# A graph attention layer with a mixture of experts: the general attention as a second pass behind the experts, and a new opening

## The chip, the cores and the metric

The kernel runs on one core of a Trainium2 chip. The metric is the device time of one execution in microseconds. The engines named below are TensorE (PE), VectorE (DVE), ScalarE (ACT), GpSimd (POOL) and SyncE (SP); each works through its own instructions in order, and SP, ACT and POOL also issue DMA transfers.

## What is computed

`x` has 4096 rows of 256 numbers, `adj` is a 4096 x 4096 matrix of 0 and 1, which the kernel gets transposed. A graph attention layer with four heads of 64 is followed by a layer of eight experts, of which each row uses its best two.

```python
# attention on n = layernorm(x); h, s_col, s_row come from n
h = jnp.einsum('nd,hdk->hnk', x, W)
s_col = jnp.einsum('hnk,hk->hn', h, a1)
s_row = jnp.einsum('hnk,hk->hn', h, a2)
e = jax.nn.leaky_relu(s_row[:, :, None] + s_col[:, None, :], negative_slope=0.2)
e = jnp.where(adj[None, :, :] > 0, e, NEG_INF)
att = jax.nn.softmax(e, axis=-1)
h_prime = jnp.einsum('hij,hjk->hik', att, h)
y = jax.nn.elu(out) + x @ Wr + br           # out: h_prime, heads side by side
x = x0 + layernorm(y) * gamma + beta        # x0: the layer's input
# experts on n = layernorm(x)
top_w, top_i = jax.lax.top_k(n @ Wg + bg, 2)     # softmax over the two
for e in range(8):
    hid = jax.nn.gelu(n @ W1[e] + b1[e], approximate=False)
    out = out + w_dense[:, e:e + 1] * (hid @ W2[e] + b2[e])
```

## The kernel before

**Stages.** An opening, the attention, the experts. The rows are cut into eight blocks of 512 (`b`, each of four tiles of 128). The attention goes over four groups of 1024 target rows (`a`), each of two halves of one block, and in each over 32 tiles of 128 source rows (`j`). For each `j` and head VectorE makes a weight tile `w` of 128 x 1024 (`weigh`, L1353), and TensorE multiplies it into the sums `acc` (L835) and the denominators `den` (L844): 24 products a step, 12 where only one half is done. Ten `w` buffers lie between the two engines.

**Separable and general form.** Where the scores stay within a limit, exp(leaky_relu(r + c)) is the larger of two products of a row factor and a column factor, so `w` is one instruction: maximum of the row factor `er` and the column factor `eb`, then minimum with the mask. Where they do not, a general form is used (maxima over the neighbours first, then the weights). Which of the two it is depends on a limit found from the weights (`scores_weights`, L551 to L557, ends in `flag`). The flag is read by every engine (L1270) and `tc.If(general > 0)` (L1275) stands in front of both forms. With these inputs the general form is never taken.

**Opening.** `norm_block(0)`: statistics, three root steps, normalised rows (L623), transposes (L630), copies that also sum the columns (L643). `scores_weights` makes the score columns of the weights by a product and a reduction on VectorE. `project_first` multiplies block 0 (L747), `store_parts` and `load_rows` (L793, L800) send its row factors through memory so that each partition gets all of them (`er`). `residual_first` (L778) computes the residual of block 0. Block 1 is normalised ahead of the branch.

**Behind the branch.** For the first four `j` the halves are done one by one, half 0 and then half 1, because block 1 has to be projected first (L695, L702) and its row factors go through memory too; `prepare_at` gives out this work. Block 2 is normalised and projected during the half-1 steps (its first piece is at step 4), blocks 3 to 7 at steps 4b to 4b+3. From `j = 4` on both halves are done. Between the steps the results of the group before are finished (`pending`). In the last group the list of the first expert tiles is made (`plan_early`, `first_tile`).

**Experts.** For each tile of an expert `fetch`, `turn`, `up` (L1519) and `down` (L1550); the sum `o` (L1561) is added into the output by an indirect DMA on POOL (L1572). Each add waits for the add before it. The last tile's two adds (`o_last0`, `o_last1`) are held back: the first (L1556) goes out when its own sum is ready, the second (L1572) behind it. A count of tiles that did not fit the plan is read, and `tc.If(further > 0)` (L1645) guards tiles beyond the fixed number; it is not taken either. The generator `giving` of the last tile is finished behind that branch: the second half's sum and add.

Of the kernel before, what the change touches and what calls it, by code (L numbers as in the profile page):

```python
# [32 lines left out]
WARM = 37  # L33
# [10 lines left out]
def gat_then_moe(  # L44
# [92 lines left out]

    def rows_of(mat, b):
        return mat[ts(b, B), :].rearrange("(t p) d -> p t d", p=P)
# [15 lines left out]
    def root_of(var, n, part=1.0, steps=3):  # L155


        v = small.tile([P, n], F32, tag="v", name="v")
        nc.vector.tensor_scalar(v, var, part, EPS, op0=OP.mult, op1=OP.add)
        r = small.tile([P, n], F32, tag="r", name="r")  # L160
        nc.vector.tensor_scalar(
            r.bitcast(I32), v.bitcast(I32), -0.5, 1597463007.0, op0=OP.mult, op1=OP.add
        )
        q = small.tile([P, n], F32, tag="q", name="q")
        for _ in range(steps):
            nc.vector.tensor_tensor(q, r, r, OP.mult)
            nc.vector.scalar_tensor_tensor(q, q, -0.5, v, op0=OP.mult, op1=OP.mult)
            nc.vector.scalar_tensor_tensor(r, q, 1.5, r, op0=OP.add, op1=OP.mult)
        return r, v
# [27 lines left out]
    moe = ctx.enter_context(tc.tile_pool(name="moe", bufs=1))  # L197
    fin = ctx.enter_context(tc.tile_pool(name="fin", bufs=1))
    ps = ctx.enter_context(tc.tile_pool(name="ps", bufs=1, space=PSUM))
    gam = fin.tile([P, D], F32)  # L200
    bet = fin.tile([P, D], F32)

    hbar = fin.tile([P, H // 2], F32)


    home = [fin]

    def large(name):
        return home[0].tile([P, TB, D], F32, tag="large", name=name, bufs=3)

    def first_large(name):
        return fin.tile([P, TB, D], F32, tag="first", name=name, bufs=2)

    def loaded(name):
        return fin.tile([P, TB, D], F32, tag="loaded", name=name, bufs=2)

    def residuals(name):
        return fin.tile([P, TB, D], F32, tag="residual", name=name, bufs=1)

    def bank(shape, name):  # L220
        return ps.tile(shape, F32, tag="bank", name=name, bufs=3)

    tiny = fin.tile([P, 1], F32)
    nc.vector.memset(tiny, TINY)

    xr0 = moe.tile([CH, 2, RW], F32)
    xT0 = moe.tile([P, DC, TT], F32)
    w10 = moe.tile([P, DC, F], F32)


    b1r = moe.tile([E * FC, P], F32)
    bT = moe.tile([P, FC, E], F32)

    def turn_biases():
        pb = bank([P, E * FC], "pb")
        order_of(nc.tensor.transpose(pb, b1r, ident[: E * FC, : E * FC]))
        nc.vector.tensor_copy(bT, pb.rearrange("p (e f) -> p f e", e=E))

    plans = [moe]

    def moe_tile(name, shape, dtype=F32):
        return plans[0].tile(shape, dtype, name=name, bufs=1)

    def tables(tag, width):

        return {
            "expert": moe_tile(f"expert{tag}", [P, width]),
            "mark": moe_tile(f"mark{tag}", [P, width]),
            "own": moe_tile(f"own{tag}", [P, width, E]),
            "place": moe_tile(f"place{tag}", [P, width]),  # L250
            "rows": moe_tile(f"rows{tag}", [P, width]),
            "float": moe_tile(f"float{tag}", [P, 2, width]),
            "int": moe_tile(f"int{tag}", [P, 2, width], I32),
            "past": moe_tile(f"past{tag}", [P, width, E]),
            "parts": 3 if tag == "w" else 2,
            "upto": moe_tile(f"upto{tag}", [P, E]),
        }

    def whole(name, n, least):

        more = moe_tile(f"more{name}", [P, E, KT])
        less = moe_tile(f"less{name}", [P, E])
        nc.vector.tensor_scalar(less, n, least, None, op0=OP.subtract)
        nc.vector.tensor_tensor(
            more, less.unsqueeze(2).to_broadcast([P, E, KT]),
            steps.unsqueeze(1).to_broadcast([P, E, KT]), OP.is_gt,
        )
        tiles = moe_tile(f"tiles{name}", [P, E])
        nc.vector.tensor_reduce(tiles, more, AX.X, OP.add)
        return tiles  # L270

    def plan(t, width, n, tiles, used):

        wide = [P, width, E]
        upto, past, own, place = t["upto"], t["past"], t["own"], t["place"]
        nc.vector.tensor_copy(upto, tiles)
        for e in range(1, E):
            nc.vector.tensor_tensor(
                upto[:, e : e + 1], upto[:, e : e + 1], upto[:, e - 1 : e], OP.add
            )  # L280
        nc.vector.tensor_tensor(
            past, upto.unsqueeze(1).to_broadcast(wide),
            num[:, :width].unsqueeze(2).to_broadcast(wide), OP.is_le,
        )
        nc.vector.tensor_reduce(t["expert"], past, AX.X, OP.add)
        nc.vector.tensor_tensor(past, past, tiles.unsqueeze(1).to_broadcast(wide), OP.mult)
        nc.vector.tensor_reduce(place, past, AX.X, OP.add)
        nc.vector.tensor_tensor(place, num[:, :width], place, OP.subtract)

        nc.vector.tensor_scalar(  # L290
            t["mark"], t["expert"], -1.0, float(E), op0=OP.mult, op1=OP.add
        )
        nc.vector.tensor_tensor(
            own, t["mark"].unsqueeze(2).to_broadcast(wide),
            order.unsqueeze(1).to_broadcast(wide), OP.is_equal,
        )
        if used is not None:
            nc.vector.tensor_tensor(
                past, own, used.unsqueeze(1).to_broadcast(wide), OP.mult
            )  # L300
            nc.vector.tensor_reduce(t["rows"], past, AX.X, OP.add)
            nc.vector.tensor_tensor(place, place, t["rows"], OP.add)
        nc.vector.tensor_scalar(place, place, float(TT), None, op0=OP.mult)
        nc.vector.tensor_tensor(past, own, n.unsqueeze(1).to_broadcast(wide), OP.mult)
        nc.vector.tensor_reduce(t["rows"], past, AX.X, OP.add)
        nc.vector.tensor_tensor(t["rows"], t["rows"], place, OP.subtract)
        table = t["float"]
        nc.vector.tensor_scalar(table[:, 0], t["expert"], float(E - 1), None, op0=OP.min)
        nc.vector.scalar_tensor_tensor(
            table[:, 1], t["expert"], float(LIST), place, op0=OP.mult, op1=OP.add  # L310
        )

        nc.vector.tensor_scalar(
            table[:, 1], table[:, 1], filled[:, E - 1 :], None, op0=OP.min
        )
        nc.vector.tensor_copy(t["int"], table)
        return t
# [104 lines left out]
    def after(ins, other, reason):  # L422
# [3 lines left out]
            reason=reason,  # L426
        )

    last = [None]

    def queue(ins):

# [1252 lines left out]
```

## Time and profile before

| | us |
|---|---|
| median of 3 runs (lowest, highest) | 1284.34 (1283.99, 1289.04) |
| the profiled execution's time | 1287.53 |
| its span in the profile | 1285.8 |
| its mean granted TensorE clock | 0.996 |
| TensorE busy | 1255.5 |
| VectorE busy | 847.7 |
| ScalarE busy | 463.3 |
| POOL busy | 239.2 |

In the profile an instruction group is given as line, engine, operation, tiles out<-in and shape, then the number of instructions. `DVEq`, `POOLq` and so on are what an engine's sequencer does itself: reads of a register, branches, events. In square brackets stands the idle time in front of an instruction and what ended it. A window's row gives the busy time of each engine in that stretch, the granted clock and the share of the DMA engines.

### The profile page before, as it was taken

What the parts mean: (1) busy time and instruction counts of PE and PEld (TensorE: products, weight loads), DVE (VectorE), ACT (ScalarE), POOL (GpSimd) and SP (SyncE); (2) the same over time, 40 slices, a digit from 0 to 9 for tenths busy, and PEclk for the clock granted to TensorE, in tenths of its full rate; (3) what the DMA queues carried; (4) which work ended last, traced back from release to release, by engine and by line L of the source; (5) the groups of instructions that cost most, each with busy time, mean ns of one, the idle gap of its engine ahead of it and who ended that gap; (6) DMA issues with size and microseconds to landing.
All of it is one profiled execution on the core that took longest, in us unless ns stands there. A gap on an engine that the chain in (4) does not pass through costs nothing.

```text
span 1285.8 us, 23209 instructions
## 1 busy us (share of the span) xinstructions
PE 1255.5 (98%) x9073; PEld 685.4 (53%) x9073; DVE 847.7 (66%) x1623; ACT 463.3 (36%) x974; POOL 239.2 (19%) x196
## 2 busy tenths in 40 slices
PE   6999999999999999999999999998999999999997
PEld 4434444332232332332322325887888877888886
DVE  5799887879999999999999994934111121111110
ACT  4313222155522365421654313532333333233232
POOL 1000000001002701007010042245222212221212
PEclk9999999999999999999999999999999999999999
DMA  6523533336533746335463325978776776787782
GB/s 204 182 84 115 190 107 115 106 134 134 187 110 105 230 112 201 101 99 164 140 176 118 101 71 196 331 200 251 218 189 162 197 183 143 199 209 194 192 210 42
DMA packets 145010, 205.84 MB, mean 160 GB/s; under 512 B 49808, under 2 KB 113952, under 8 KB 144240
## 3 DMA queue, kind: packets, MB, share of 16 engines
q1 hardware_dynamic: 122432, 161.26, 40.8%
q0 software_dynamic: 20224, 35.68, 12.4%
q10 hardware_dynamic: 2224, 7.22, 1.6%
q8 instruction: 76, 1.25, 0.4%
q14 instruction: 54, 0.44, 0.1%
HBM read 171.89 MB, written 29.08 MB: 156 GB/s over the span
## 4 chain that ended last, share of the span: by engine, by line
PE 70%; DVE 6%; DMA 1%; issue 1%; SPq 1%; ACT 0%; POOLq 0%; DVEq 0%; ACTq 0%
PE acc L835 23%; PE po L1550 17%; PE ph L1519 17%; PE den L844 11%; DVE w L1353 4%; DMA early<-lists 1%; PE ptx L890 1%; PE pt L494 1%; PE ptr L1122 0%; PE pl L901 0%; DMA out<-o_last,ids 0%; SPq L1135 0%; SPq L1136 0%; POOLq L1681 0%; PE pd L1038 0%
## 5 line engine op out<-in xcount | busy, mean ns | idle before, releaser
L835 PE MATMUL acc<-w,ha 128*32 128x512 f32 x4096 | 670.4, 594 | 0.9 <-ACT u L1032 0.9
L1353 DVE SCALAR_TENSOR_TENSOR w<-er,eb,am 128x1024 f32<-128x1024 f32 x496 | 604.5, 1276 | 29.4 <-PE den L844 21.9
L844 PE MATMUL den<-w,unit 128*2 128x512 f32 x2048 | 465.5, 594 | 10.7 <-DVE w L1353 9.1
L835 PEld LDWEIGHTS acc<-w,ha 128*32 128x32 f32 x4096 | 182.2, 110 | 297.9 <-issue 265.2
L1236 ACT ACTIVATE am<-adj 128x1024 bf16<-128x1024 int32 x124 | 130.8, 1055 | 362.1 <-DVE w L1353 218.9
L1519 PE MATMUL ph<-xT,w 128*128 128x256 f32 (+1 forms) x1056 | 241.3, 386 | 4.3 <-DVE xT L498 3.1
L1550 PE MATMUL po<-w,hT 128*128 128x256 f32 x1088 | 240.2, 379 | 0.0
L1523 ACT ACTIVATE hT<-ph,bias 128x256 f32<-128x256 f32 (+1 forms) x264 | 126.2, 480 | 294.5 <-PE ph L1519 207.1
L1519 PEld LDWEIGHTS ph<-xT,w 128*128 128x128 f32 x1056 | 200.0, 190 | 40.2 <-DVE xT L498 3.5
L1550 PEld LDWEIGHTS po<-w,hT 128*128 128x128 f32 x1088 | 205.5, 190 | 27.7
L1561 DVE SCALAR_TENSOR_TENSOR o<-po,share,b2s 128x256 f32<-128x256 f32 x66 | 31.8, 482 | 261.0 <-PE po L1550 242.8
L844 PEld LDWEIGHTS den<-w,unit 128*2 128x2 f32 x2048 | 93.5, 85 | 163.0 <-issue 157.2
L1572 POOL DMA_INDIRECT out<-o,ids x66 | 103.0, 1561 | 334.1 <-DVE o L1561 157.3
L1016 POOL DMA_INDIRECT lists<-xe,at x64 | 93.6, 1463 | 267.0 <-issue 182.3
L498 DVE COPY xT<-pt 128x256 f32<-128x256 f32 x12 | 5.1, 424 | 61.3 <-PE pt L494 61.3
L725 POOL DMA_DIRECT2D residual<-rb x7 | 5.5, 779 | 159.2 <-DVE rb L720 136.6
L1542 ACT ACTIVATE b2s<-b2b,share 128x256 f32<-128x256 f32 x68 | 30.8, 503 | 0.0
L695 PE MATMUL ph<-wall,xT 128*128 128x264 f32 x112 | 28.8, 400 | 0.7 <-ACT xT L643 0.7
L695 PEld LDWEIGHTS ph<-wall,xT 128*128 128x128 f32 x112 | 20.0, 189 | 15.1 <-issue 8.7
L1072 POOL DMA_DIRECT2D xf<-in_x x6 | 8.1, 1345 | 100.3 <-ACT xf L1071 54.8
L702 PE MATMUL pr<-wr,xT 128*128 128x256 f32 x112 | 26.5, 379 | 0.0
L1353 DVE SCALAR_TENSOR_TENSOR w<-er,eb,er 128x512 f32<-128x512 f32 x32 | 22.3, 744 | 5.6 <-issue 5.6
(348 smaller groups left out, 632.7 us busy)
## 6 DMA issues: line engine op xcount, KB each, us to landing
w<-in_L_ffn_W SPq DMA_DIRECT2D x66, 1024.0 KB
adj<-in_adj SPq DMA_DIRECT2D x126, 512.0 KB
er<-parts ACTq DMA_DIRECT2D x3, 2048.0 KB
b2b<-in_L_ffn_b SPq DMA_DIRECT2D x33, 128.0 KB
early<-lists SPq DMA_DIRECT2D x16, 260.0 KB
residual<-rb POOLq DMA_DIRECT2D x8, 512.0 KB
rb<-residual SPq DMA_DIRECT2D x8, 512.0 KB
out<-y POOLq DMA_DIRECT2D x8, 512.0 KB
```

The source lines that it names most:

```text
L695: order_of(nc.tensor.matmul(phs[t - t0], xT[:, c, ts(t, P)], wall[:, c, :], start=(c == 0), stop=(c == DC - 1),))
L835: queue(nc.tensor.matmul(acc[half][h // 2][here : here + Q, :], ha[:, j, h * K + g * Q : h * K + (g + 1) * Q], w[half][h], start=(j == 0), ...
L844: queue(nc.tensor.matmul(den[here : here + HB, :], unit[:, j, h, 1 - half : 1 - half + HB], w[half][h], start=(j == 0 and half == 0), stop ...
L1016: ins = nc.gpsimd.indirect_dma_start(lists, bass.IndirectOffsetOnAxis(ap=at[:, k, t : t + 1], axis=0), xe[:, t, :], None,).ins
L1236: nc.scalar.activation(am, at, AF.Relu, scale=2.0)
L1353: nc.vector.scalar_tensor_tensor(wh[:, these], er[:, these, h], eb[:, j, h : h + 1], mask[:, these], op0=OP.max, op1=OP.min,)
L1519: order_of(nc.tensor.matmul(ph, job["w1"][:, c, ts(f, P)], xT[:, c, :], start=(c == 0), stop=(c == DC - 1),))
L1523: job["gelu"] = nc.scalar.activation(hT[:, f, :], ph, AF.Gelu, bias=job["bias"][:, f : f + 1]).ins
L1542: nc.scalar.activation(b2s[k], b2b, AF.Identity, scale=share[:, k : k + 1])
L1550: order_of(nc.tensor.matmul(po, hT[:, f, ts(k, CH)], w2[:, f, :], start=(f == 0), stop=(f == FC - 1)))
L1561: given_out.append(nc.vector.scalar_tensor_tensor(o, po, share[:, k : k + 1], b2s[k], op0=OP.mult, op1=OP.add).ins)
L1572: add()
```

## The change

The attention and the experts move into one function `forward(apart, stack)`. The program calls `forward(True, ctx)`, the separable form, with no branch in front of it. The old flag becomes `strayed`; it is carried into the table of counts, and its maximum with the other two conditions is what the branch at the end reads. In that branch stand the further tiles, and, under a second condition, `forward(False, again)`, the whole general pass, after which the two last sums are set to zero. The two last adds stand behind the branch.

```diff
+    held, further, held_back, last_sums = forward(True, ctx)
+    with tc.If(held(2, 1) > 0):
+        further()
+        with tc.If(held(3, 1) > 0):
+            with ExitStack() as again:
+                held, further, rest_of_sums, _ = forward(False, again)
+                with tc.If(held(2, 1) > 0):
+                    further()
+                for add in rest_of_sums:
+                    add()
+            for o in last_sums:
+                nc.vector.memset(o, 0.0)
+    for add in held_back:
+        add()
...
-    with tc.If(further > 0):
...
-    next(giving, None)
...
             if k + 1 == nch:
                 yield
-                while job["last"] and held_back:
-                    held_back.pop(0)()
             if job["last"]:
-                o = work.tile([CH, D], F32, name=f"o_last{k}", bufs=1)
+                o = kept.tile([CH, D], F32, name=f"o_last{k}")
+                last_sums.append(o)
...
-            if job["last"] and k + 1 < nch:
+            if job["last"]:
                 held_back.append(add)
```

The opening is new. `first_phase(weigh)` writes its instructions in an order by hand, and `in_trace_order` ties each engine to that order. The score weights come from TensorE (`heads_made`, `weights_turned`, `scores_weights`). The rows are only centred before they are transposed, and their factor `r` is applied behind the products (`of_tile`, `scaled`, `residual_kept`). The limits use no root step and a factor of 1.09 in place of one step and 1.01. The row factors of blocks 0 and 1 are spread over the partitions by 16 transposes each and four copies (`spread_parts`), not through memory; blocks 2 to 7 go through memory as before. The column sums of blocks 0 and 1 are 16 products with one moving column (`sums_of_centred`). Block 1's root steps run on POOL. The warm-up products go from 37 to 9 and 3.

```diff
-        warm_up(WARM)
...
-        norm_block(0)
-        second = rows_loaded(1)
-        with tc.issue_after(marks["off"]):
-            scores_weights()
-        project_first()
...
-        with tc.If(general > 0) as chosen:
...
+            def sums_of_centred(xb, r):
+
+                po = bank([P, DC], "po")
+                for c in range(DC):
+                    for t in range(TB):
+                        order_of(nc.tensor.matmul(
+                            po[:, c : c + 1], xb[:, t, ts(c, P)], r[:, t : t + 1],
+                            start=(t == 0), stop=(t == TB - 1),
+                        ))
+                return po
...
+            def spread_parts(part, er):
 
+                for h in range(H):
+                    pe = bank([P, B], "pe")
+                    for t in range(TB):
+                        order_of(nc.tensor.transpose(
+                            pe[:, ts(t, P)], part[:, h, t : t + 1].to_broadcast([P, P]), ident
+                        ))
+                    ins = nc.scalar.copy(er[:, h], pe).ins
+                return ins
...
+            def first_phase(weigh):
...
+                warm_up(9)
+                heads_made()
+                warm_up(3)
...
+                spread_parts(part, er0[:, 0])
+                factors(0, slice(2, TB), scs[0])
...
+                heads_added(0)
+                rb = residuals("rb")
+                sums_first = [residual_products(0, t0) for t0 in (0, 2)]
...
+                for t in range(TB):
+                    centred(second, mvs[1], t)
...
+                roots_of_pool(vs[1], rs[1])
...
+                heads_added(1)
...
+                heads_added(2)
...
+                heads_added(3)
...
+                residual_pair(1, rb, 0)
+                marks["eb"] = spread_parts(part, er0[:, 1])
+                residual_pair(1, rb, 2)
+                nc.gpsimd.dma_start(rows_of(residual, 1), rb)
+                pos = [sums_of_centred(xb, r) for xb, r in ((first, rs[0]), (second, rs[1]))]
+                for b in range(HB):
+                    nc.vector.tensor_copy(sums[:, :, b], pos[b])
+
+            def roots_of_pool(v, r):
+
+                q = small.tile([P, TB], F32, tag="qp", name="qp")
+                for sign in (1, 1, -1):
+                    nc.gpsimd.tensor_tensor(q, r, r, OP.mult)
+                    nc.gpsimd.tensor_tensor(q, q, v, OP.mult)
+                    nc.gpsimd.tensor_scalar(q, q, -0.5 * sign, 1.5 * sign, op0=OP.mult, op1=OP.add)
+                    nc.gpsimd.tensor_tensor(r, r, q, OP.mult)
```

Block 2 is projected during steps 4 to 7 with both halves; so far it was during the half-1 steps. Three groups of VectorE and ScalarE work get a mark behind which they are placed.

```diff
-                    for b in range(1, NB):
-                        first = {1: 0, 2: TB}.get(b, TB * b)
-                        if b > 1 and first - 3 <= s < first:
+                        for b in range(2, NB):
+                            first = TB * b
+                            if first - 3 <= s < first:
...
-                        if first <= s < first + (3 if b == 1 else 4):
+                            if first <= s < first + 4:
...
+                with tc.issue_after(marks["top"]):
+                    found = measured(b, fetched.pop(b))
...
+                with tc.issue_after(marks["eb"]):
                 mask_of(at[:, 0], am)
...
                 for j in range(TB):
-                    am = first_masks[:, j]
-                    if j > 1:
-                        mask_of(first_adj[:, j - 2], am)
-                    attend(weigh(er, am, j, [0]), j, [0])
-                    prepare_at(j)
-                    if j == 2:
-                        load_rows(er[:, 1:], 1, 1, nc.sync)
-                for j in range(TB):
                     prepare_at(TB + j)
                     attend(weigh(er, first_masks[:, j], j, [1]), j, [1])
```

In the built program's order VectorE has, behind its copy of the column sums, the rest of the half-1 `w`, the statistics of block 2 and six `w` of the steps 4 and 5 ahead of block 2's row offset (`off`). TensorE has block 2's transposes ahead of the last half-1 step. On SP the loads of the last blocks' residuals and rows, which stood behind the end of the branch's region, stand among the adjacency loads. The first of the last two adds waits for VectorE's event behind the jump over the branch, because the block that is jumped over writes the sums too.

## The prediction

> **What bounds the kernel now.** I read the busy shares first, then the windows of the opening and of the join between attention and experts, then two timelines of the opening, and last the chain and the branch at the very end.
>
> ```profile
> PE 1255.5 (98%) x9073; PEld 685.4 (53%) x9073; DVE 847.7 (66%) x1623; ACT 463.3 (36%) x974; POOL 239.2 (19%) x196
> ...
> L1353 DVE SCALAR_TENSOR_TENSOR w<-er,eb,am 128x1024 f32<-128x1024 f32 x496 | 604.5, 1276 | 29.4 <-PE den L844 21.9
> ```
>
> TensorE sets the time over almost the whole span. A shift of its stream early on is carried to the end, because a full attention step costs TensorE 24 instructions of 0.2146 us, 5.15 us, against four w on VectorE at a pitch of 1.2 us, 4.8 us. So only the places where TensorE is idle can give time: the opening, the join and the end.
>
> ```profile
> 10.00:20.00 10.00, 8.51 (x45) 5.95 (x43) 8.28 (x44) 6.13 (x14) 0.00 (x0) 1.00 0.68 260
> 20.00:30.00 10.00, 3.83 (x22) 3.21 (x20) 3.76 (x11) 4.32 (x10) 0.79 (x1) 0.92 0.50 167
> 30.00:40.00 10.00, 9.16 (x44) 4.75 (x48) 9.29 (x25) 3.33 (x6) 0.00 (x0) 0.74 0.82 275
> ...
> 50.00:60.00 10.00, 7.23 (x48) 4.13 (x40) 3.92 (x10) 3.76 (x10) 0.00 (x0) 1.00 0.49 164
> ...
> 29.28 3.40 DVE L1353 SCALAR_TENSOR_TENSOR w<-er,eb,er 128x512 f32<-128x512 f32 x5 [5.59 <-issue]
> ...
> 30.84 1.02 PE L844 MATMUL den<-w,unit 128*2 128x512 f32 x2 [7.00 <-DVE w L1353]
> ...
> 54.86 0.17 DVE L711 TENSOR_TENSOR sc<-ph,limits 128x8 f32<-128x8 f32 x1 [4.61 <-PE ph L695]
> ```
>
> In a window row the columns are PE, PEld, DVE, ACT and POOL busy, clock, DMA share, GB/s. The first gap is the branch: the row factors' load leaves at 22.42, all engines resume at 29.0 to 29.3, and TensorE starts attention at 30.84 after 7.0 us. The clock is then low: 0.50 in 30 to 34, 0.68 in 34 to 36. The second gap, 51.2 to 59.5 with a block's projection in it, is block 1's factors going through memory. From 72.1 (first step with both halves) TensorE is full, and block 2 has been projected by then.
>
> ```profile
> 790.00:800.00 10.00, 8.68 (x48) 7.40 (x47) 5.00 (x32) 3.10 (x8) 0.00 (x0) 1.00 1.01 351
> ...
> 810.00:820.00 10.00, 8.73 (x47) 7.59 (x46) 9.72 (x36) 5.53 (x8) 1.22 (x2) 1.00 1.06 339
> ...
> L1645 DVEq EVENT_SEMAPHORE  x2: 21/21/21, 1277.7 to 1277.8; - x2
> ...
> L1645 POOLq COMPARE_BRANCH  x1: 53/53/53, 1266.1 to 1266.1; - x1
> ...
> L1645 DVEq COMPARE_BRANCH  x1: 72/72/72, 1274.8 to 1274.8; - x1
> ...
> 1274.39 0.49 DVE o_last L1561
> 1274.88 0.27 issue
> 1275.15 3.72 DMA out<-o_last,ids
> ...
> 1277.95 0.48 DVE L1561 SCALAR_TENSOR_TENSOR o_last<-po,share,b2s 128x256 f32<-128x256 f32 x1 [3.08 <-DVEq L1645]
> ```
>
> At the join TensorE loses 1.32 and 1.27 us while the DMA share is above 1. At the end the first held-back add leaves at 1275.15, as soon as its own sum is there. VectorE's jump, compare at 1274.8 and its next event at 1277.7, lies under TensorE's last product, which ends at 1277.73.
>
> **The opening, part by part.** Removed: the flag's read and branch, seven idle us; two products and two reductions of 0.69 and 0.68 on VectorE; block 0's and block 1's trips through memory (a 1 MB load each). Added on TensorE: score weights (a few transposes of 0.13 us), 32 transposes that spread the row factors, and 16 products with one moving column (column sums, so far an accumulating output of ScalarE's copies).
>
> First attention product. Rows arrive at 5.4 as now (5.47). Four statistics pairs (0.43 and 0.18), weights copied by ScalarE (0.60), centred rows (0.59 each) and their transposes bring the first projection to 10.9, the limits' chain to 13.7 (dependent small operations every 0.20), scores and factors to 16.05, spread transposes and four copies of 0.60 to 17.4 to 19.05, first w at 17.45: TensorE at about 18.9 instead of 30.84.
>
> TensorE's work from there to the end of the new opening, in its built order: four half steps of 2.58 (10.3); residual products of two blocks, 2 x 3.64 (half a projected pair with its residual takes 1.82: 64.79 to 66.61); eight transposes 1.05; block 1's products 3.76 (two pairs of 1.88); 16 spread transposes 2.1; 16 column products. The trace has no row of this last kind; the nearest is the limits' product, also 128x128 weights and a few columns, 0.31 us an instruction. From below a transpose bounds it (0.13), from above two weight loads of 0.19. I take 0.31: 5.0 us (2.1 to 6.1). Sum 29.5: the opening's last product ends at 48.4, and VectorE's copy of the sums, which waits for it, at 48.8.
>
> What is late next. VectorE is in order, and behind that copy it has, before it makes block 2's row offsets: 11 half w (0.665 each, 7.3), block 2's statistics (2.3), 11 small root operations (1.9), then six full w of the steps j=4 and j=5 (7.2), a statistic of block 3 and the offset itself (0.6). That is 19.3 us, so 68.1. TensorE's order puts block 2's transposes in front of the last half-1 step. It has only three half steps and runs dry near 56 to 58. ScalarE normalises four rows by 70.2, the last transposes take 0.25, the half step 2.58: the first full step can start at 73.0, against 72.1. The idle ten us are longer than the 7.0 that were followed by half clock for about 4 us; the first 1.5 us of that are transposes paced by ScalarE, and the rest costs 1.35. So 74.4. And block 2, now projected in j=4 to 7, still owes two pairs of 3.70 (62.91 to 66.61): 7.4. The opening costs 74.4 + 7.4 - 72.1 = **+9.7 us**.
>
> Bounds: if VectorE never waited, its work from 17.45 to the offset (32 half w 21.3, six full 7.2, statistics 5.1, small ones 4.6, 14 operations of 0.42 for ha and residuals 5.9) is 44 us, offset at 61.5, first full step at 66.4 warm: +1.7. From above: the 12 root operations now on POOL have no row there beside a DMA issue and its memsets; at 0.13 to 0.67 each (an iota, and an estimate five times that) they add 0 to 2: +11.7.
>
> The clock in the new opening is a cost of its own. The 37 warm-up products become 12, and before, the product pitch falls from 0.43 to 0.21 only at 4.6. A page speaks against the cut: the Trainium skill, "TensorE: Matmul & The Clock Gate", Part 1, has the clock fall to half after one idle window of about 3.4 us and rise only after about 3.4 us of sustained work, and the sparse products of 6 to 19 us might not be that. By the rule the opening could be half-clocked there; by the trace's row for the first 30 us (0.92 to 1.00) it is not.
>
> **The join.** No branch region ends there, so the loads of the last blocks' residuals and rows (2 MB) go earlier, between adjacency loads on SP; each is behind a store that ended several steps before, and an adjacency tile has about 15 us of slack (three mask buffers of 5.15), which hides it. TensorE loses about 3 us around 790 to 820 now. Bounds -3 to +1 (a copy and one more wait on VectorE); I take **-1**, since the weights' own loads still fill the DMA.
>
> **The end.** Both last sums now come ahead of the branch, and both adds behind it. The block that is jumped over writes those sums too, so the built add waits for VectorE's event behind the jump. POOL is queued behind that wait with both adds. VectorE's last sum runs 1277.95 to 1278.43; its read of the count takes 0.4 beside it (1274.4 to 1274.8 now), compare to event 2.9, POOL's issue 0.2: the first add leaves at 1281.4 instead of 1275.15, and the second and the span's end follow it: **+6.2 us**. From below POOL's own jump took 0.4 us (its next event is at 1266.5; +3.7), from above TensorE's 3.9 (+7.2). A page would price it otherwise: the Trainium skill, "Advanced Engine Details and Errata", Control Flow Timing, gives a compare-and-branch about 108 ns, which would make the end +3.5 and the total about 1296.5. VectorE's own 2.9 us decides.
>
> Sum: 9.7 - 1.0 + 6.2 = +14.9. Against the profiled execution (1287.53, span 1285.8, 1.7 around it) that is 1302.4. That execution lies 3.2 above the median of the runs shown, 1284.34, so against the median it is 1299.2.
>
> **Rivals.** A: VectorE sets the new opening without waiting, as at the lower bound. For it: VectorE is 80% busy in the first 100 us, and its w may run ahead of TensorE. Against: its sums copy sits behind TensorE's last opening product. 1284.3 + 1.7 - 1 + 6.2 = 1291.2.
>
> B, the other side: TensorE never runs dry in the opening. This needs block 2's offset before about 56. Then 48.4 + four half steps 10.3 + transposes 1.05 + owed 7.4 = 67.2, which is -4.9; with join and end as above 1284.6, and 1280 if both are at their lower bounds. For it: the branch's seven us are really gone. Against: 11 half and six full w stand ahead of the offset.
>
> C: half clock between 6 and 19. Some 7 us of TensorE work lie there on the chain; at 0.5 they cost 3.5 to 7: 1303 to 1306.
>
> D: the jump is short, as POOL's: 2.5 less, 1296.7, inside the forecast.
>
> **How the numbers follow.** The forecast with D, 1293 to 1303, has 0.52; A 0.22; B 0.14; C 0.12. The time is the forecast's, 1299. The range 1287 to 1305 takes in A, most of C and leaves out most of B and a rest. About 0.5%, 6.4 us, is what a measurement can tell: same is 1277.9 to 1290.8. Faster: the low end of B with the first add released earlier than I read it, 0.04, and 0.01 for the rest. Same: what is left of B (0.10), half of A (0.11) and 0.02 of the forecast, 0.23. Slower: 0.72.
>
> **What would show it.** Opening: first attention product near 19; a wait of block 2's transposes on ScalarE of some 10 us before 70; the first full step near 74 with block 2's projection behind it; a low clock around 70. End: the first add some 3 us behind the last sum, released by VectorE's queue. The forecast is wrong if that gap is under 3 us, if TensorE's first full step comes before 67, or if the idle time at the join grows.

## The result and the profile after

| | before | after | difference |
|---|---|---|---|
| median of 4 runs each (lowest, highest), us | 1285.63 (1283.99, 1289.04) | 1302.64 (1302.38, 1303.19) | ratio 1.0129, 95% interval 1.0106 to 1.0152 |
| profiled execution: time, span | 1287.53, 1285.8 | 1302.63, 1301.0 | +15.2 in the span |
| first attention product begins | 30.84 | 19.21 | -11.6 |
| end of the first attention group | 266.75 | 274.06 | +7.3 |
| TensorE's last product ends | 1277.73 | 1286.26 | +8.5 |
| span ends | 1285.8 | 1301.0 | +15.2 |

The new kernel is slower. Read downwards, the last column tells where: attention begins 11.6 us earlier, by the end of the first group the kernel is 7.3 us behind, between there and the last product 1.2 us are added, and 6.7 more behind it. The end of the first group is read from one product that has the same idle time in front of it in both kernels. Here are its lines, from TensorE's timelines of the kernel before and, in the second fence, of the kernel after (start, duration, engine, line; the idle time and its releaser in brackets):

```profile
266.75 0.62 PE L835 MATMUL acc<-w,ha 128*32 128x512 f32 x2 [0.93 <-ACT u L1032]
```

```profile
274.06 0.62 PE L1090 MATMUL acc<-w,ha 128*32 128x512 f32 x2 [0.92 <-ACT u L1287]
```

I call the time from the first attention product to this one the first group. It was 235.91 us and is now 254.85: 18.9 us more, of which 11.6 had been won ahead of it. It holds more work than before (projections and residuals that used to lie ahead of the first product), but the windows of the kernel after show that work is only part of it:

```profile
40.00:50.00 10.00, 9.90 (x78) 8.19 (x80) 6.76 (x14) 4.99 (x7) 0.78 (x1) 1.00 0.30 87
50.00:60.00 10.00, 7.00 (x60) 1.90 (x52) 9.16 (x25) 0.00 (x0) 0.00 (x0) 1.00 0.63 229
60.00:70.00 10.00, 2.47 (x12) 1.36 (x16) 9.65 (x30) 3.61 (x6) 0.00 (x0) 0.51 0.16 52
70.00:80.00 10.00, 10.00 (x74) 2.58 (x67) 7.15 (x9) 3.79 (x9) 0.00 (x0) 0.81 0.32 100
```

TensorE (first column after the width) is full until 57, busy for 2.47 us of the ten from 60 to 70, and then runs at a granted clock of 0.81 on average. VectorE (third) is full in just that stretch. The timeline of the kernel after has the chain behind it:

```profile
44.81 3.63 PE L782 MATMUL po<-rrow,xb 128*128 128x1 f32 x32
46.68 2.17 SPq L663 DMA_DIRECT2D xb<-in_x  x2
...
52.78 0.43 DVE L187 BATCH_NORM_STATS2 st<-xb 128x6 f32<-128x256 f32 x1 [0.84 <-DMA xb<-in_x]
...
66.64 0.15 DVE L674 SCALAR_TENSOR_TENSOR off<-mv,r 128x4 f32<-128x4 f32 x1
66.87 2.08 ACT L682 ACTIVATE xb<-xb,off,r 128x256 f32<-128x256 f32 x4 [1.96 <-DVE off L674]
67.53 2.17 PE L689 MATMUL pt<-ident,xb 128*128 128x128 f32 x8 [10.53 <-ACT xb L682]
```

The column sums (`po<-rrow,xb`) read the row tiles of block 0 and then of block 1, from 44.8 to 48.4. Block 2's rows go into block 0's buffer, so their load is issued only at 46.68, half-way through, and VectorE's statistics on them begin at 52.78. SP's queue has a share in that: in front of this load it has one of the adjacency matrix, which waited 24.1 us for ScalarE's masks and was issued at 44.90. Behind it, block 2's load waited another 1.4 us for the products. The offset comes at 66.64, behind six full `w`, and TensorE has waited 10.53 us for what ScalarE makes of it. The first step with both halves starts at 74.29 (72.1 before).

The end of the kernel after: the last sum on VectorE, then what the sequencers did at the branch (count, shortest/median/longest in ns, first and last start), then the first add.

```profile
1286.37 0.48 DVE L1784 SCALAR_TENSOR_TENSOR o_last<-po,share,b2s 128x256 f32<-128x256 f32 x1 [2.97 <-PE po L1774]
1290.25 1.55 POOL L1904 DMA_INDIRECT out<-o_last,ids_last  x1 [14.35 <-DVEq L1892]
```

```profile
L1892 POOLq EVENT_SEMAPHORE  x6: 17/30/587, 1277.3 to 1278.3; - x6
...
L1892 DVEq EVENT_SEMAPHORE  x2: 21/21/21, 1290.0 to 1290.1; - x2
...
L1892 DVEq COMPARE_BRANCH  x1: 76/76/76, 1287.1 to 1287.1; - x1
```

VectorE compares at 1287.1, when its last sum is done, and its next event is at 1290.0. POOL's last event of its own jump starts at 1278.3; it has been idle for 14.35 us, the last part of them waiting for VectorE's event with both adds behind it. The first add leaves 3.4 us after the last sum (1286.85); before, it left under TensorE's last product.

### The profile page after: what moved, and what is told of

Its sections match the earlier page's. It is cut to its first block, busy times and chain, and to the rows that moved or that the text cites. A ratio compares the mean times of both kernels' runs of the same rounds, so it can differ in the third digit from the quotient of the medians.

```text
span 1301.0 us, 23254 instructions
## 1 busy us (share of the span) xinstructions
PE 1261.3 (97%) x9117; PEld 692.2 (53%) x9117; DVE 849.2 (65%) x1617; ACT 466.5 (36%) x977; POOL 237.2 (18%) x215
## 5 line engine op out<-in xcount | busy, mean ns | idle before, releaser
L1271 POOL DMA_INDIRECT lists<-xe,at x64 | 86.0, 1344 | 267.0 <-issue 182.9
L945 PE MATMUL pr<-wr,xT 128*128 128x256 f32 x128 | 30.3, 381 | 0.0
L945 PEld LDWEIGHTS pr<-wr,xT 128*128 128x128 f32 x128 | 24.1, 190 | 5.0 <-issue 0.9
L993 PE MATMUL ph<-wall,xT 128*128 128x264 f32 x96 | 24.6, 399 | 0.0
L197 ACT ACTIVATE m<-y,off 128x256 f32<-128x256 f32 x48 | 23.7, 494 | 1.1 <-DVE off L205 0.6
```

Of the source, the lines that this page charges most:

```text
L945: order_of(nc.tensor.matmul(pr[:, k, :], turned[b][:, c, ts(t0 + k, P)], wr[:, c, :], start=(c == 0), stop=(c == DC - 1),))
L1271: ins = nc.gpsimd.indirect_dma_start(lists, bass.IndirectOffsetOnAxis(ap=at[:, k, t : t + 1], axis=0), xe[:, t, :], None,).ins
```

## The experiments

My theory has two places. In the opening TensorE waits because block 2 comes late, for two reasons that can be undone apart: where its offset stands in VectorE's order, and how long the column sums hold the row buffers. At the end VectorE's jump stands in front of both adds. The rivals: the added work of TensorE itself is the loss; the half clock is; the join is. Ratios are against the kernel before, run on the same chip. Because executions of one kernel spread by several us in the experts, the opening is judged by the length of the first group: in the profiles of three executions whose opening is that of the kernel after, it is 254.85, 253.84 and 254.28.

**e1: POOL zeroes the last sums in the block that is jumped over.**

```diff
-                nc.vector.memset(o, 0.0)
+                nc.gpsimd.memset(o, 0.0)
```

> One word differs from the changed kernel: in the branch at the end the two last sums are set to zero by POOL instead of VectorE (the branch is not taken). Theory (the first held-back add waits for VectorE's event behind the jump, only because VectorE writes the sums in the jumped-over block): the add's wait becomes the last sum alone, so it leaves some 0.3 us behind that sum instead of 3.4, and the second add and the end follow: the gap from TensorE's last product to the span's end falls from 14.7 to about 11 us and the time from 1302.6 to about 1299. The remaining 3 us against before would then be the first add, which can now leave only behind the second sum. Rival (everything behind the branch is late, whoever writes): within 1 us of 1302.6. Second rival (the whole 6.7 us is the jump): 1296.

Measured: 1296.18, ratio 1.0081 (1.0046 to 1.0116). The first add is no longer released by VectorE, but in the profiled execution it was late all the same, for another reason:

```profile
1270.11 1.55 POOL L1795 DMA_INDIRECT out<-o,ids  x1 [2.97 <-DMA out<-o,ids]
1274.62 1.55 POOL L1795 DMA_INDIRECT out<-o,ids  x1 [2.96 <-DMA out<-o,ids]
1275.98 0.48 DVE L1784 SCALAR_TENSOR_TENSOR o_last<-po,share,b2s 128x256 f32<-128x256 f32 x1 [9.89 <-PE po L1774]
...
1282.48 1.55 POOL L1904 DMA_INDIRECT out<-o_last,ids_last  x1 [6.31 <-issue]
```

Each indirect add waits for the one before it, 4.5 us apart. Here POOL still had an ordinary add to issue at 1274.62 and only then came to its own jump (one event there lasted 2.33 us). The span ended 14.0 us behind the last product, nearly as with the wait on VectorE (14.7). The timed runs lie between 1288.75 and 1304.7. By their ratio the edit is worth 0.3 to 0.5% against the kernel after (1.0081 beside 1.0112 in e6 and 1.0129), 4 to 6 us, but the intervals overlap and the profile shows less than 1 us of gain at the end: alone it decides nothing. The same edit is in e5, e8 and e10 to e12.

**e2: block 2's offset ahead of the w of the first full steps**, by order alone.

```diff
-                                weigh(er, load_mask(a, j), j, both), j, both,
+                            am = load_mask(a, j)
+                            with tc.issue_after(marks["off2"]):
+                                ws = weigh(er, am, j, both)
...
+                                ws, j, both,
```

> The w of the steps with both halves are placed behind block 2's row offset on VectorE. Theory (six full w stand ahead of the offset and TensorE waits for it): the offset comes at about 62 instead of 66.6, TensorE's wait falls from 10.5 to about 6 us, first full step near 69.5 instead of 74.3; time about 1298. Rival A (the six w only move: VectorE's lead of six w, which now lets TensorE run steps 4 to 8 unpaced, is lost and costs 2.3 again): 1300. Rival B (the late load of block 2's rows sets it): 1302.6, no change.

Measured: 1295.83, ratio 1.0068 (1.0045 to 1.0092); first group 248.59, 6.3 us shorter. The timeline:

```profile
59.33 0.16 DVE L674 SCALAR_TENSOR_TENSOR off<-mv,r 128x4 f32<-128x4 f32 x1
...
60.32 2.17 PE L689 MATMUL pt<-ident,xb 128*128 128x128 f32 x8 [4.83 <-ACT xb L682]
```

The offset is 7.3 us earlier (5.9 if both are counted from the first attention product, which came at 17.84 here), as it no longer stands behind six `w`, and the wait falls from 10.53 to 4.83. The order is about one half of the cause; the rest of the wait needs another.

**e3: the column sums early, and block 2's rows loaded behind the first of them.** VectorE's order of `w` and offset is left to follow from that.

```diff
+                pos = [sums_of_centred(first, rs[0])]
+                fetched[2] = rows_loaded(2)
...
+                pos.append(sums_of_centred(second, rs[1]))
...
-                pos = [sums_of_centred(xb, r) for xb, r in ((first, rs[0]), (second, rs[1]))]
```

> The same column-sum products, but block 0's directly behind block 1's transposes and block 1's ahead of the third half step, and block 2's rows are loaded directly behind the first of them. Theory (the sums at the end of the opening hold both row buffers until 48, so block 2's rows come at 52.6 and its offset falls behind half-1's and six full w): the rows come before 38, the offset near 54, TensorE's 10.5 us wait falls to 1 or 2 and the clock stays up; first full step near 61 to 62; VectorE then paces steps 4 to 8 (2.3 back): 10 to 11 us less, about 1292. Rival (only VectorE's order counts, as in the run that moves the w): about 1298. Rival (the work is conserved, the wait moves to VectorE's w): 1301 or more.

Measured: 1292.64, ratio 1.0027 (0.9999 to 1.0054); first group 243.06, 11.8 us shorter than after, with the same instructions on TensorE.

```profile
26.47 1.95 PE L782 MATMUL po<-rrow,xb 128*128 128x1 f32 x16 [0.24 <-ACT xT L802]
28.45 8.48 SPq L663 DMA_DIRECT2D xb<-in_x  x2
...
56.23 0.15 DVE L674 SCALAR_TENSOR_TENSOR off<-mv,r 128x4 f32<-128x4 f32 x1
...
57.60 1.43 PE L689 MATMUL pt<-ident,xb 128*128 128x128 f32 x8
```

The load leaves at 28.45 in place of 46.68, the offset is there at 56.23, and the transposes carry no bracket: there is no wait. In SP's queue the load now also stands in front of the adjacency load that was ahead of it; no run moved it there alone, or the products alone. The 11.8 us are as much as the wait of 10.5 and the 1.35 that the prediction had put down for the half clock after it. So most of what the opening loses is this wait, and the rival that TensorE's added work is the loss falls: with that work unchanged the first group ends at 261.34, 5.4 us before that of the kernel before.

**e5: e1 and e3 together.**

> Both of the above: POOL zeroes the last sums and the column sums are early. If the two terms are independent, the sum of both gains: about 1288 to 1289 by my numbers for each, and within 1 us of what the two single runs add up to. If the ends share a cause (a later stage absorbs part), it is more than 1 us above that sum.

Measured: 1282.19, ratio 0.9954 (0.9932 to 0.9975): faster than the kernel before and, by the ratios, 1.6 to 1.7% faster than the kernel after (1.0112 in e6, 1.0129). First group 243.07 again. At the end:

```profile
1270.24 0.48 DVE L1783 SCALAR_TENSOR_TENSOR o_last<-po,share,b2s 128x256 f32<-128x256 f32 x1 [9.89 <-ACTq L1891]
1271.52 1.55 POOL L1903 DMA_INDIRECT out<-o_last,ids_last  x1 [5.63 <-DVE o_last L1783]
```

The first add leaves 0.8 us behind its own sum (1270.72), under TensorE's last product, and the span ends 8.62 us behind that product, against 14.74 after and 8.07 before. The two single edits took 0.0048 and 0.0102 off the ratio 1.0129; together that would be 0.998. The pair gives 0.9954, some 3 us below their sum, where the expectation allowed 1 us; that e1 did not get the end back in its profile fits this. The edit does not always do so: over the six profiles that have it, the span ends 8.6 to 8.8 us behind the last product in e5, e8 and e10, but 14.0 in e1, 11.5 in e11 and 10.9 in e12. There POOL issues its last ordinary add only 4.7 to 6.3 us ahead of the last product's end (9.2 to 11.9 in the other three), comes to its own jump late, and the first add leaves 1.1 to 1.2 us behind that jump's last record.

**e6: the kernel after once more**, on the chip of the next three.

> The changed kernel once more, beside the kernel before on the same chip as the next three. Theory: it stays slower by some 15 us (span 1301 against 1286), whatever the chip: ratio 1.010 to 1.014. Rival (part of the 17 us belonged to the first chip or to that one execution): under 1.008.

Measured: 1296.94 against 1282.06, ratio 1.0112 (1.0098 to 1.0127). That is inside the theory's 1.010 to 1.014. The wait is there with 9.5 us, the first add again waits for VectorE's event. In its opening something else happened, in the first of these windows:

```profile
10.00:15.00 5.00, 4.73 (x15) 3.86 (x16) 2.64 (x19) 2.17 (x4) 4.31 (x7) 0.57 1.00 396
15.00:20.00 5.00, 4.22 (x17) 3.12 (x17) 1.66 (x7) 0.58 (x4) 0.00 (x0) 0.75 0.58 197
60.00:70.00 10.00, 0.81 (x8) 0.00 (x0) 10.00 (x23) 1.41 (x2) 0.00 (x0) 0.76 0.10 24
```

The granted clock is 0.57 in 10 to 15 (1.00 in the first profile of the same kernel), and the first attention product begins at 22.03, not 19.21.

**e7: the kernel before with the new end alone.** Both sums ahead of the branch, the zeroing in it, both adds behind it.

```diff
-                while job["last"] and held_back:
-                    held_back.pop(0)()
...
+    next(giving, None)
...
+        for o in last_sums:
+            nc.vector.memset(o, 0.0)
...
-    next(giving, None)
+    for add in held_back:
+        add()
```

> The kernel before with the new end alone: both last sums ahead of the branch, VectorE zeroes them inside it (not taken), both adds behind it; opening and join as before. Theory (the add waits for VectorE's event behind the jump): the first add leaves some 3.5 us behind the second sum, 6 to 7 us later than now, and the span grows by as much: 6.0 to 6.9 us. Rival A (the end of the changed kernel is late for another reason, its far larger block or a later POOL): 0 to 1 us. Rival B (only the wait for the second sum counts, the jump runs beside it): 3.3 us.

Measured: 1289.02, ratio 1.0053 (1.0040 to 1.0066), which is 6.8 us of 1282.06. The span ends 14.61 us behind the last product. Its lines are those of the kernel after:

```profile
1272.80 0.48 DVE L1560 SCALAR_TENSOR_TENSOR o_last<-po,share,b2s 128x256 f32<-128x256 f32 x1 [2.97 <-PE po L1550]
1276.64 1.54 POOL L1658 DMA_INDIRECT out<-o_last,ids  x1 [14.26 <-DVEq L1645]
```

So the new end costs 6.8 us with the old opening too. The run moves the sums and adds and writes the zeros at once; how much of it the write alone is worth, only e1 and e5 bear on.

**e4: the kernel after without the column-sum products.** POOL sets those sums to zero; the mean that a row without neighbours takes then lacks blocks 0 and 1.

```diff
-                pos = [sums_of_centred(xb, r) for xb, r in ((first, rs[0]), (second, rs[1]))]
-                for b in range(HB):
-                    nc.vector.tensor_copy(sums[:, :, b], pos[b])
+                nc.gpsimd.memset(sums[:, :, :HB], 0.0)
```

> The changed kernel without the 32 records of column-sum products; POOL sets these two blocks' sums to zero, so the mean used for rows without neighbours lacks blocks 0 and 1. Theory (the products matter by holding the row buffers, and their own 3.6 us of TensorE are on the path only in part): block 2's rows come before 36, the 10.5 us wait is gone, the first full step comes at 58 to 61, so 0 to 3.6 us below the run with early sums, 10 to 14 us below the changed kernel. Rival (only their own TensorE time counts): 3.6 us below the changed kernel, 1299.

Measured: 1278.17, ratio 0.9965 (0.9952 to 0.9977), with the slow end kept; first group 238.24. Against e3 that is 4.8 us, more than the 0 to 3.6 expected: the products' own price and what goes with them. In the kernel after they fill 44.8 to 48.4, 3.6 us for both blocks. Together with e3 this divides the 16.6 us that the products cost in the kernel after: 11.8 for where they stand, 4.8 for what they are. Nothing else was edited here, yet block 2's rows leave at 11.06: without the products the built order has their load in front of the adjacency loads that stand ahead of it in the kernel after. So what the late products cost comes by both, the buffer that they hold and the place in SP's queue that the load gets by it, and the runs do not part the two.

**e8: block 2 brought still further forward.** e5, with block 2 measured, normalised and turned at the end of the opening and projected in the half-1 steps, as the kernel before did.

```diff
+                found = measured(2, fetched.pop(2))
...
+                for t in range(TB):
+                    normal_row(found, t)
+                turn_block(2, found[0])
...
-                            first = TB * b
+                            first = TB if b == 2 else TB * b
```

> As the run with early sums and POOL's zeroing, and block 2 is measured, normalised and turned at the end of the opening and projected during the half-1 steps, as the kernel before did. Theory (the 7.4 us that block 2 owed in steps 4 to 7 now lie where TensorE is short of w): first full step at 66 to 68 with block 2 done, against 63.0 plus 7.4 owed; 2 to 4 us below the run with both edits, ratio to before 0.992 to 0.994. Rival (VectorE paces the half-1 steps and the steps 4 to 8 anyway, so the work only moves): the same as that run within 1 us.

Measured: 1282.58, ratio 1.0008 (0.9995 to 1.0021); first group 247.12, 4 us longer than in e5. The expectation failed. Here is the same window in e5 and, in the second fence, in e8:

```profile
80.00:100.00 20.00, 20.00 (x168) 7.72 (x167) 20.00 (x38) 7.07 (x15) 1.31 (x2) 1.00 0.46 151
```

```profile
80.00:100.00 20.00, 18.89 (x172) 5.53 (x164) 20.00 (x34) 7.46 (x12) 0.00 (x0) 1.00 0.42 129
```

VectorE is full in both, TensorE only in e5. All of the 4 us are lost by block 3's projection, which begins 82.1 us after the first attention product, against 78.1 in e5. Two are waits of TensorE for ScalarE, 1.08 us for block 2's copies (at 53.03) and 0.95 for block 3's rows (at 93.11); the rest falls where TensorE counts as busy. The chain to block 2's offset now holds VectorE from 42.7 to 48.3, in front of most of the half-1 `w`. That this keeps VectorE from building the lead of `w` that would carry the first full steps fits these rows, but it is argued, not shown.

**e9: the kernel before without its branch.** Only the front branch and the general form are taken out; the opening stays as it was.

```diff
-        general = nc.values_load(
...
-        with tc.If(general > 0) as chosen:
+        if False:
...
-        with chosen.Else():
+        if True:
```

> The kernel before with its front branch and the general form taken out (the flag is still computed, nobody reads it; scores outside the limit would come out wrong), all else as it was: the worth of the branch alone, with the old opening. Theory (the 7.0 us gap is the branch's fetch on top of the row factors' load, issued at 22.4, which would itself hold the first w until some 26): first attention product near 27 instead of 30.8, the gap of 7 falls to 3, the clock stays up (2 us of half speed less), and the group's end moves from 266.7 to about 262: 4 to 6 us less. Rival A (the load is landed long before, the whole gap goes): 7 to 9 us less. Rival B (the later gap, block 1's trip through memory at 51 to 59, takes the gain up): under 1.5 us.

Measured: 1291.13, ratio 1.0071 (1.0057 to 1.0086): slower, on the side that none of my cases had. The timeline:

```profile
18.33 1.06 ACT L1236 ACTIVATE er<-er 128x1024 bf16<-128x1024 int32 x1 [6.26 <-DMA er<-in_adj]
...
20.02 6.66 PE L747 MATMUL acc<-wall,xT 128*128 128x264 f32 x16 [6.05 <-ACT xT L643]
...
31.01 0.33 SPq L800 DMA_DIRECT2D er<-parts  x1
...
38.68 2.74 DVE L1349 SCALAR_TENSOR_TENSOR w<-er,eb,er 128x512 f32<-128x512 f32 x4 [5.50 <-DMA er<-parts]
...
40.15 1.02 PE L844 MATMUL den<-w,unit 128*2 128x512 f32 x2 [8.07 <-DVE w L1349]
```

With the branch gone, ScalarE has an adjacency mask (L1236), work from behind it, ahead of the copy that TensorE's first projection waits for. The projection starts at 20.02, the row factors' load is issued at 31.01 (22.42 before), and attention begins at 40.15, 9.3 us later than with the branch. So the branch had kept later work out of the opening. How much of the seven idle us in front of attention was its own is not shown: without it the first `w` starts 7.7 us after the issue of the row factors' load and waits for that load, and TensorE's gap is 8.07; in the kernel before the first `w` started 6.9 us after that issue. That the changed kernel gains 11.6 us there comes with an order written by hand (`in_trace_order`); removing the branch did not do it.

**e10: e5 with cheaper column sums.** The products read the upper 16 bits of the rows and a 16-bit factor that POOL makes, in one pass. These sums serve only the mean for rows without neighbours.

```diff
+                rough = small.tile([P, TB], BF16, tag="rough", name="rough")
+                nc.gpsimd.tensor_copy(rough, r)
+                high = xb.rearrange("p t d -> p (t d)").bitcast(BF16)
+                high = high.rearrange("p (t d k) -> p t d k", t=TB, k=2)[:, :, :, 1]
...
-                            po[:, c : c + 1], xb[:, t, ts(c, P)], r[:, t : t + 1],
+                            po[:, c : c + 1], high[:, t, ts(c, P)], rough[:, t : t + 1],
```

> As the run with both edits (early sums, POOL zeroes), and the column-sum products read the rows' upper 16 bits as bf16, with a bf16 copy of the factor: a single pass each in place of two, for a mean that only rows without neighbours use. Theory (the run without the products was 4.8 us ahead of the one with early sums from the first attention product to the end of the first group, so their TensorE time lies wholly on the path): half of their time or more saved, 2 to 4 us below the run with both edits, ratio to before 0.992 to 0.994, and the group's end 240 us behind the first attention product in place of 243. Rival (VectorE paces the opening once the sums are early): no gain, 0.995 to 0.996.

Measured: 1275.06 against 1280.99, ratio 0.9954 (0.9936 to 0.9972); first group 239.23, 3.8 us shorter than e5. By the ratio alone this is the rival's case (0.995 to 0.996, no gain); by the first group it is the theory's (240 expected). The two kernels ran on different chips, hence e11 and e12. The eight products of a block now take 0.34 us, and wait 1.20 us for the factor that POOL makes:

```profile
28.84 0.34 PE L786 MATMUL po<-rough,xb 128*128 128x1 bf16 x8 [1.20 <-POOL rough L781]
```

**e11 and e12: the kernels of e5 and e10, unchanged, on one chip.**

> The run with both edits (early sums, POOL zeroes) again, on one chip with the next run, since the two had the same ratio to before on different chips. Theory (both terms undone leave the new opening ahead of the old): ratio below 1 again, 0.993 to 0.998. Rival: 1 within its interval.

> The run with both edits and the one-pass sums again, beside the run before it. Theory (the products' time lies on the path, 242.1 us from the first attention product to the group's end without them and with early two-pass sums 243.1): 2 to 4 us below the run beside it. Rival (a later stage takes it up, as equal ratios on two chips would have it): within 1 us of it.

Measured against 1282.34: 1280.93, ratio 0.9986 (0.9963 to 1.0009), and 1276.29, ratio 0.9947 (0.9922 to 0.9972). The 4.6 us between them are a little more than expected; by the first groups (243.06 and 239.22) it is 3.8. In the expectation of e12, "242.1 us" for the kernel without the products is a slip: that first group was 238.24. For the kernel of e5 alone this run is the rival's case: 1 lies within the interval. The kernel of e5 was faster in one of two comparisons, the kernel of e10 in both. The latter is the best found: 0.5% ahead of the kernel before and 1.6 to 1.8% ahead of the kernel after, by the ratios.

## Why the prediction was right

The time, 1299, was 3.6 us low and the direction right. The total is closer than its terms: +9.7, -1.0 and +6.2 were put down, and the span shows +7.3, +1.2 and +6.7, so that the opening's error is made up by the stretch behind it, 14.9 against 15.2. That is luck. By its steps:

**The opening's chain, right.** First attention product near 19: 19.21. The opening's last product at 48.4: the next attention product starts at 48.37. The wait of "some 10 us": 10.53. The first full step at 74.4: 74.29. Two pairs of errors cancelled on the way. The column products were over-priced (5.0 us taken, 3.6 measured), while the four half steps in front of them took 11.5 us where the sum had 10.3. And the offset was there at 66.8, 1.3 us sooner than the sum's 68.1, while the transposes and the half step behind it ran at a clock of 0.50 until about 73: that half step took 4.67 us where the sum had 3.93 with its allowance for the clock.

**The opening's sum, right in mechanism, 2.4 us too large.** "74.4 + 7.4 - 72.1 = +9.7" took the 7.4 us that block 2 still owes as carried to the end. At the end of the first group the loss is 7.3, and it is 7.3 already at block 3's projection (first product at 109.04, 101.73 before). In 80 to 100 VectorE was busy 20.00 of 20 before and is busy 16.23 after:

```profile
80.00:100.00 20.00, 20.00 (x192) 6.28 (x184) 20.00 (x21) 6.31 (x9) 0.00 (x0) 1.00 0.41 129
```

```profile
80.00:100.00 20.00, 20.00 (x154) 9.22 (x156) 16.23 (x26) 4.12 (x9) 0.75 (x1) 1.00 0.25 83
```

The six `w` that VectorE made while TensorE waited are a lead. With it TensorE runs through these steps at its own pace, where before it went at VectorE's. That part of the stall paid itself back is argued from these rows and, more weakly, from e8; no run changed the lead alone.

**The cause, half named.** "Behind that copy it has ... 19.3 us" put the lateness on VectorE's order. e2 shows that this is worth 6.3 us, and e3, which has no wait left, that the late rows are worth 11.8; the two overlap. The row buffers that the column products hold, and the place of the rows' load in SP's queue, were not in the text, though they lay in the built kernel: the load waited for the buffer's last reader (46.68, in the middle of the products). The number came out right because the statistics' place in VectorE's order and the arrival of the rows fell together: VectorE waited only 0.84 us for them (the line at 52.78). That they did is luck too.

**The join, -1, not seen.** From the end of the first group to the start of the last expert product it was 1003.91 before and 1005.13 after. Executions whose stage is the same program gave 1000.09 (e6), 999.94 (e7) and 997.8 to 1008.81 in the others. The term cannot be told from zero within a spread of some 10 us. At the join itself, from 780 to 840, TensorE is idle for 2.8 us before and for 2.6 after, so the term's own place gained 0.2 in these two profiles, not 1.

**The end, +6.2, right:** +6.7 in the profile, +6.8 by e7's ratio, undone in the profiles of e5, e8 and e10. The page's price for a compare-and-branch (the Trainium skill, "Advanced Engine Details and Errata", Control Flow Timing, about 108 ns) would, by an estimate, have made it +3.5; VectorE's 2.9 us from compare to next event, the same in both kernels, was the one to take. D falls with it. The bound from below was wrong as a reading. POOL's first event came 0.4 us after its compare in the kernel before, but one event behind it lasted 2.92 us:

```profile
L1645 POOLq EVENT_SEMAPHORE  x5: 17/43/2920, 1266.5 to 1269.8; - x5
```

From the compare to the start of the last event POOL took 3.7 us there (1266.1 to 1269.8) and 3.8 in the kernel after (1274.5 to 1278.3). What the long event waited for is not shown, but 0.4 us was not the whole of POOL's way through the branch.

**The rivals.** A and B fall: VectorE did wait for the rows, and TensorE ran dry. e3 is what B described, and it ends with the first group 5.4 us ahead, against B's -4.9. C is partly real. Of the eleven profiles with the new opening, four had a clock of 0.50 to 0.68 in 10 to 15 us (e4, e5, e6, e10) and began attention at 19.7 to 22.0; the other seven had 1.00 and began at 17.8 to 19.2. The page behind it (the Trainium skill, "TensorE: Matmul & The Clock Gate", Part 1) says that the clock rises only after sustained work, and these profiles agree that 12 warm-up products are a close thing: the three profiles of the old opening, with 37, all had 1.00 there (before, e7, e9). The new opening with more of them was not tried.

## What to carry to other kernels

When products are appended as the last readers of a buffer, price who is to be loaded into that buffer next: 3.6 us of column sums cost 16.6, because the next block's rows waited for them. A cheap write inside a block that is normally jumped over can put that engine's jump in front of a later reader; let the engine that reads write it, and see to it that this engine comes to its own jump early. And a branch that is never taken may still be what keeps later work out of an opening: take it away only together with an order.

## What the runs showed of the hardware

A jump over code that is not run is not short here: from VectorE's compare to its next event 2.9 us in before, after and e5; TensorE's weight queue's compare itself lasted 3.8 us in before, 3.5 in the kernel after and 4.4 in e1; from POOL's compare to the start of its last event at the branch it was 3.7 us in before and e5, 3.8 in after and 5.4 in e1. What the longer events wait for the profile does not say.

The granted clock of one program differed between executions in the same stretch: 1.00 and 0.57 in 10 to 15 us of the kernel after, with TensorE busy 4.33 and 4.73 of the 5 us. What decides it is open.

A product with one moving column is cheap but not free. In full precision each is two records: the eight products of a block took 1.95 us (the 16 records at 26.47 in e3), 0.24 each, where the prediction took 0.31 from the nearest row. The eight in 16 bits, one record each, took 0.34, 0.04 each.
